# Second graph layer of a GNN kernel: own products moved into the loop of the neighbour sums, transposes two tiles later, the convolution spread over that loop, the output bias added later

## The chip, the cores and the metric

The kernel runs on one core of one Trainium2 chip. The metric is the device time of one execution in microseconds (us). The core has a matrix engine (TensorE, PE in the profile), a vector engine (VectorE, DVE), a scalar engine (ScalarE, ACT), GpSimd (POOL) and a queue that issues transfers (SyncE, SP). Each engine takes its own instructions strictly in the order of the program and waits for the others by semaphores.

## The reference, cut to what matters

The whole program is a graph layer, an attention and expert layer, a second graph layer and a second attention layer over 1250 nodes of width 512. The change touches the second graph layer and what prepares the second attention. In reduced form:

```
h   = layernorm(x)
own = h @ W_self.T
agg = A @ (h @ W_neigh.T) / deg            # A: 1250 x 1250 counts of edges
u   = own + agg + bias1
x   = x + layernorm(u) * gamma + beta
g   = layernorm(x)                         # second attention layer
c   = g + conv3(g, pos_w) + pos_b          # along the nodes, per channel
q, k, v = split(c @ qkv_w.T + qkv_b)
x   = x + attention(q, k, v) @ wo_w.T + wo_b
```

Everything is float32. The sums with A are exact in a split form: `h @ W_neigh.T` is kept as two parts, nb_hi and nb_lo, whose sum is the value.

## The kernel before, in words

The nodes lie in T = 10 tiles of P = 125 rows, the 512 channels in K = 4 blocks of 128. X holds x by rows. Four stages follow each other here; the times are those of the profiled execution.

1. The experts of the layer before (until 925 us) end with X complete.
2. The products loop (L1336 to L1347, 931 to 1007 us). A scheduler orders this part. For each tile: normalise a row tile (L639), transpose it on TensorE (L850), copy it out (L1341), multiply it by w_m and split the result into nb_hi (ScalarE, L646) and nb_lo (VectorE, L647), multiply it by w_s and add bias1 into the tile `slot` (L1347). GpSimd adds beta to X (L1339).
3. The sums' loop (L1414 to L1423, 1007 to about 1079 us), in an order written out by hand. In step t: ScalarE casts the counts of the next tile (cast1, L1359). TensorE sums 20 products of counts with nb_hi and nb_lo (adj_sum1, L861). VectorE joins the sum with the own product (L1365) and takes its statistics (L631 to L634). ScalarE takes the root (L635) and scales (L1375), and GpSimd multiplies by gamma and adds into X (scale1_, L1376 and L1377). The statistics and the normalisation of the finished X come two tiles later (stats1 and normed1), its transposition onto TensorE three tiles later (turn1_, L850 and L1393), with two copies of one column each by VectorE (L1397, L1398) that give every tile its neighbours' edge columns. GpSimd adds the output bias wo_b to X there (L1392). The convolution of tiles 0 and 1 (conv1: one ScalarE and two VectorE instructions for a channel block, L1407 to L1409) stands in step 5.
4. The projections (L1459 to L1466, until 1184 us): convolution of tiles 2 to 5, then q, k and v of tiles 0 and 1, convolution of tiles 6 to 9, then q, k and v of tiles 2 to 5 and of 6 to 9. TensorE's results go through three PSUM buffers (ps_mm); VectorE reads out q (L1443) and v (L1457), ScalarE and VectorE the two parts of k (L1449, L1450).

The second attention begins after that and takes the rest of the time. PSUM has three buffers for products (ps_mm), two for transposes (ps_tp) and two for sums (ps_o); the pool `work` keeps two of each of its tiles (h, u, the statistics). Weights share three SBUF buffers, so w_k and w_v of the second attention are loaded when w_m and w_s have been read for the last time.

Of the kernel before, what the change touches and what calls it, by code (L numbers as in the profile page):

```python
# [9 lines left out]
F32 = mybir.dt.float32  # L10
# [5 lines left out]
AF = mybir.ActivationFunctionType  # L16
ALU = mybir.AluOpType
# [3 lines left out]
P = 125  # L21
T = N // P
D = 512
K = D // 128
# [548 lines left out]
def tile_usual(ctx: ExitStack, tc: tile.TileContext, a: dict, out: bass.AP):  # L573
    nc = tc.nc
# [7 lines left out]
    def close(*pools):  # L582
        for p in pools:
            p.__exit__(None, None, None)
# [35 lines left out]
    X = keep.tile([P, T, D], F32, name="X")  # L620
    atu_pool, atu = pool("atu", 1, "left")

    CT = atu.tile([P, T, N], F16, name="CT")
    deg = keep.tile([P, T], F32, name="deg")
    edges = keep.tile([P, 1], F32, name="edges")

    def stats(pool, x):
        st = pool.tile([P, 6], F32, name="st")
        mv = pool.tile([P, 2], F32, name="mv")
        rs = pool.tile([P, 1], F32, name="rs")  # L630
        nc.vector.bn_stats(st, x)  # L631
# [3 lines left out]
        nc.scalar.sqrt(rs, rs)  # L635
        return mv, rs
# [35 lines left out]
    qk_b = cols(a["qk_b"], "qk_b")  # L672
    w_q = load_w(a["Wq"], "w_q")
# [58 lines left out]
    with (  # L732
# [73 lines left out]
        late, banks, touched, hs, hTs = [], {}, {}, {}, {}  # L806
# [9 lines left out]
        for r in range(rounds):  # L816
# [7 lines left out]
            while order and (order[0][0] <= r or r == rounds - 1):  # L824
                _, i, t = order.pop(0)
# [8 lines left out]
    def ps_mm():  # L834
        return psum.tile([128, 512], F32, tag="mm", name="ps_mm")
# [4 lines left out]
    def ps_o():  # L840
        return psum.tile([128, 512], F32, tag="o", name="ps_o", bufs=2)
# [4 lines left out]
    def transposed(x):  # L846

        ps = ps_tp()
        for k in range(K):
            nc.tensor.transpose(ps[:, k * P : (k + 1) * P], x[:, k * 128 : (k + 1) * 128], ident[:P, :P])  # L850
        return ps[:, : K * P].rearrange("p (k n) -> p k n", k=K)

    def product(ps, xT, t, w):

        for k in range(K):
            nc.tensor.matmul(ps, xT[:, k, span(t, t + 1)], w[:, k, :], start=(k == 0), stop=(k == K - 1))

    def summed(ps, ad):

        for n, (t, part) in enumerate((t, part) for t in range(T) for part in (nb_hi, nb_lo)):  # L860
            nc.tensor.matmul(ps, ad[:, t, :], part[:, t, :], start=(n == 0), stop=(n == 2 * T - 1))  # L861
# [177 lines left out]
    with (  # L1039
# [147 lines left out]
        for i in (1, 3):  # L1187
            r = slice(i * E, (i + 1) * E)
# [53 lines left out]
    with tc.tile_pool(name="moe", bufs=2, side="right") as moe:  # L1242
# [89 lines left out]

    slot = slots.tile([128, T, D], F32, name="slot")
    hT = slot[:, :, : K * (P + 2)].rearrange("p t (k n) -> p t k n", k=K)
    w_q = load_w(a["qkv"][:, :D], "w_q1")
    for t in range(T):  # L1336
        h = work.tile([P, D], F32, name="h")
        norm(h, X[:, t, :])
        nc.gpsimd.tensor_add(X[:, t, :], X[:, t, :], beta1)  # L1339
        xT = work.tile([128, K, P], F32, tag="xT4", name="hT1")  # L1340
        nc.scalar.copy(xT, transposed(h))  # L1341
        ps = ps_mm()
        product(ps[:P], xT, 0, w_m)
        split(nb_hi[:, t, :], nb_lo[:, t, :], ps[:P])
        ps = ps_mm()
        product(ps[:P], xT, 0, w_s)
        nc.vector.tensor_add(slot[:P, t, :], ps[:P], bias1)  # L1347
    w_k = load_w(a["qkv"][:, D : 2 * D], "w_k1")
    w_v = load_w(a["qkv"][:, 2 * D :], "w_v1")

    manual = tc.manual_schedule()
    manual.__enter__()
    xT = xc.tile([128, K, N], F32, name="xT")
    us, hs = {}, {}

    def cast1(t):
        if t < T:
            ads[t] = adj.tile([P, T, P], F32R, name="ad1")
            nc.scalar.copy(ads[t], CT[:, :, span(t, t + 1)])  # L1359

    def adj_sum1(t):
        agg = ps_o()
        summed(agg[:P], ads.pop(t))
        u = work.tile([P, D], F32, name="u")
        nc.vector.scalar_tensor_tensor(u, agg[:P], deg[:, t : t + 1], slot[:P, t, :], op0=ALU.mult, op1=ALU.add)  # L1365
        mv, rs = stats(work, u)
        us[t] = (u, mv, rs)

    def scale1_(t):
        if not 0 <= t < T:  # L1370
# [8 lines left out]
    def stats1(t):  # L1379
        if 0 <= t < T:  # L1380
            hs[t] = stats(work, X[:, t, :])

    def normed1(t):
        if 0 <= t < T:
            h = work.tile([P, D], F32, name="h")
            normed(h, X[:, t, :], *hs[t])
            hs[t] = h

    def turn1_(t):
        if not 0 <= t < T:  # L1390
            return
        nc.gpsimd.tensor_add(X[:, t, :], X[:, t, :], wo_b)  # L1392
        nc.scalar.copy(hT[:, t, :, 1 : P + 1], transposed(hs.pop(t)))  # L1393
        if t == 0:
            nc.vector.memset(hT[:, t, :, 0:1], 0.0)
        else:
            nc.vector.tensor_copy(hT[:, t, :, 0:1], hT[:, t - 1, :, P : P + 1])  # L1397
            nc.vector.tensor_copy(hT[:, t - 1, :, P + 1 : P + 2], hT[:, t, :, 1:2])  # L1398
        if t == T - 1:
            nc.vector.memset(hT[:, t, :, P + 1 : P + 2], 0.0)  # L1400

    def conv1(t0, t1):

        for k in range(K):
# [3 lines left out]
            nc.vector.scalar_tensor_tensor(c, at[:, :, :P], pos_w[:, k, 0:1], c, op0=ALU.mult, op1=ALU.add)  # L1408
            nc.vector.scalar_tensor_tensor(c, at[:, :, 2:], pos_w[:, k, 2:3], c, op0=ALU.mult, op1=ALU.add)  # L1409
# [3 lines left out]
    cast1(0)  # L1413
    for t in range(T + 3):  # L1414
        cast1(t + 1)
        if t < T:
            adj_sum1(t)
        stats1(t - 2)
        scale1_(t)
        normed1(t - 2)  # L1420
        turn1_(t - 3)
        if t - 3 == 2:
            conv1(0, 2)  # L1423
    close(work_pool, adj_pool, g1_pool, atu_pool)


    qkv1_pool, qkv1 = pool("qkv1", 1, "left")
# [3 lines left out]
    K2 = qkv1.tile([128, H, N], F32R, name="K2")  # L1431
    V = qkv1.tile([P, T, D], F32, name="V1")

    def project1_(t0, t1):
        n = (t1 - t0) * P
        for w in (w_q, w_k):
            for f in range(K):
                ps = ps_mm()
                for k in range(K):
                    nc.tensor.matmul(ps[:, :n], w[:, k, f * 128 : (f + 1) * 128], xT[:, k, span(t0, t1)],  # L1440
                                     start=(k == 0), stop=(k == K - 1))
                if w is w_q:
                    nc.vector.tensor_scalar(qT[:, f, span(t0, t1)], ps[:, :n], qk_b[:, f : f + 1],  # L1443
                                            float(D) ** -0.5, op0=ALU.add, op1=ALU.mult)
                    continue
                for i, (own, other) in enumerate(PAIRS):
                    hi, lo = (K2[r, 2 * f + i, span(t0, t1)] for r in (own, other))
                    b = qk_b[own, K + f : K + f + 1]
                    nc.scalar.activation(hi, ps[own, :n], AF.Identity, bias=b)  # L1449
                    nc.vector.scalar_tensor_tensor(lo, ps[own, :n], b, hi.bitcast(F32),  # L1450
                                                   op0=ALU.add, op1=ALU.subtract)
# [351 lines left out]
```

## Time and profile before

| what | value |
|---|---|
| time, median of 3 runs | 1625.26 us (1623.89 to 1626.26) |
| time of the profiled execution | 1624.99 us |
| its span from first to last instruction | 1623.1 us |
| TensorE busy | 1456.4 us, 90% |
| VectorE busy | 897.3 us, 55% |
| ScalarE busy | 706.6 us, 44% |
| GpSimd busy | 443.1 us, 27% |

The busy shares are means over stages with different limits. For this change the stretch from 931 us (first w_m product) to 1184 us (last v product) is what counts, and in it the time in which TensorE waits. A row of the timeline gives the start, the duration, the engine, the line, the operation with its tiles, and in brackets the idle time before it with what ended it. A float32 product of one tile appears as eight TensorE records.

### The profile page before, as it was taken

Reading aid. Unit: us, or ns where it says so; the run is one execution under the profiler, and the core shown is the slowest. Engines: PE = TensorE matmul, PEld = TensorE weight load, DVE = VectorE, ACT = ScalarE, POOL = GpSimd, SP = SyncE. Lnnn points to the kernel's source line nnn. Section 1 sums busy time; section 2 is a strip of 40 time slices with the busy share of each in tenths; the row PEclk is TensorE's granted clock in tenths of the full one; section 3 lists DMA queues with packets and bytes.
Section 4 is the critical chain, followed back from the end, with each engine's and each line's share of the span. In section 5 each row is a group of like instructions: output and inputs, shape, how many; then the busy total and the mean of one; then the engine's idle time right before and its main releaser. Section 6 shows DMA issues by size and latency. Waiting matters only on the chain. (4 is left out here: it accounts for less than half of the span.)

```text
span 1623.1 us, 21508 instructions
## 1 busy us (share of the span) xinstructions
PE 1456.4 (90%) x8133; PEld 954.3 (59%) x8133; DVE 897.3 (55%) x1413; ACT 706.6 (44%) x1334; POOL 443.1 (27%) x634
## 2 busy tenths in 40 slices
PE   4999998868888998999999899879978999999995
PEld 2566744447777776444444445654456777777773
DVE  5985556634433332411222332764278889999992
ACT  2333433335555553111100111432157888888882
POOL 0110000011111111000000010540057888887872
PEclk8999999979999999999999999989989999999998
DMA  4001000010101010010000201000100000000000
GB/s 133 25 1 52 1 1 1 0 42 16 40 15 44 19 25 14 29 50 26 26 26 27 83 0 52 1 0 1 36 16 14 14 20 20 21 20 21 20 8 22
DMA packets 41666, 39.82 MB, mean 25 GB/s; under 512 B 25717, under 2 KB 30063, under 8 KB 41553
## 3 DMA queue, kind: packets, MB, share of 16 engines
q1 hardware_dynamic: 41553, 38.36, 8.1%
q8 instruction: 66, 1.08, 0.3%
q14 instruction: 47, 0.39, 0.1%
HBM read 25.51 MB, written 2.56 MB: 17 GB/s over the span
## 5 line engine op out<-in xcount | busy, mean ns | idle before, releaser
L1573 POOL TENSOR_TENSOR e<-e,sg 125x1250 f32<-125x1250 f32 x80 | 206.0, 2576 | 34.3 <-ACT sg L1570 33.2
L1285 DVE SCALAR_TENSOR_TENSOR X<-ps_o,gate,X 125x512 f32<-125x512 f32 x80 | 60.1, 751 | 192.5 <-PE ps_o L1283 192.5
L1521 PE MATMUL S<-K,stacks 128*125 128x512 f32 (+1 forms) x480 | 126.0, 387 | 30.7 <-ACT sg L1570 29.9
L1583 PE MATMUL ps_t<-ident,e 125*125 125x125 f32 x800 | 135.6, 293 | 12.4 <-ACT R L1624 6.0
L1283 PE MATMUL ps_o<-we,hid 128*125 128x512 f32 x320 | 141.0, 595 | 0.0
L1590 ACT ACTIVATE pT<-ps_t 125x500 f32<-125x500 f32 x200 | 117.9, 589 | 47.8 <-PE ps_t L1583 46.9
L1583 PEld LDWEIGHTS ps_t<-ident,e 125*125 125x125 f32 x800 | 108.6, 191 | 48.0 <-ACT pT L1590 27.5
L1535 DVE MAX8 best<-S 125x8 f32<-125x1250 f32 x80 | 116.9, 1462 | 34.8 <-PE S L1521 33.5
L1275 PE MATMUL ps_mm<-yT,we 128*128 128x500 f32 (+1 forms) x352 | 127.6, 521 | 0.3 <-DVE gate L1183 0.3
L1278 ACT ACTIVATE hid<-ps_mm,b 128x500 f32<-128x500 f32 (+1 forms) x44 | 26.9, 611 | 220.6 <-PE ps_mm L1275 220.6
L1555 DVE MAX8 best<-rest 125x8 f32<-125x1250 f32 x80 | 117.1, 1464 | 2.8
L1546 DVE MATCH_REPLACE8 rest<-best,S 125x1250 f32<-125x1250 f32 x80 | 116.0, 1450 | 0.0
L1060 PE MATMUL S<-K,stacks 128*125 128x512 f32 (+10 forms) x288 | 87.1, 413 | 29.9 <-ACT e L1082 25.3
L1570 ACT ACTIVATE sg<-S,below 125x1250 f16<-125x1250 f32 x80 | 104.8, 1310 | 18.0 <-POOL below L1556 18.0
L1639 PE MATMUL O<-pT,V 125*64 125x125 f32 x1600 | 112.6, 279 | 0.0
L1521 PEld LDWEIGHTS S<-K,stacks 128*125 128x125 f32 x480 | 76.3, 193 | 52.1 <-ACT sg L1570 36.2
L1563 ACT ACTIVATE e<-S,nm 125x1250 f32<-125x1250 f32 x80 | 104.1, 1302 | 2.3 <-DVE rest L1546 1.1
L1108 ACT COPY pT<-ps_t 125x500 f32<-125x500 f32 (+3 forms) x112 | 54.9, 490 | 113.9 <-PE ps_t L1103 113.4
L1339 POOL TENSOR_TENSOR X<-X,beta 125x512 f32<-125x512 f32 x10 | 13.4, 1359 | 329.0 <-DVE h L639 328.3
L1275 PEld LDWEIGHTS ps_mm<-yT,we 128*128 128x128 f32 x352 | 66.9, 191 | 61.0 <-issue 58.6
L1283 PEld LDWEIGHTS ps_o<-we,hid 128*125 128x125 f32 x320 | 59.2, 187 | 71.6 <-issue 71.3
L990 POOL TENSOR_TENSOR stacks<-yT,stacks 64x125 fp32r<-64x125 f32 x80 | 34.1, 426 | 230.0 <-ACT stacks L989 226.6
(225 smaller groups left out, 2669.7 us busy)
## 6 DMA issues: line engine op xcount, KB each, us to landing
we<-in_W SPq DMA_DIRECT2D x16, 512.0 KB
stacks<-stacks SPq DMA_DIRECT2D x160, 31.2 KB
stacks<-stacks SPq DMA_DIRECT2D x40, 125.0 KB
X<-in_x SPq DMA_DIRECT2D x5, 500.0 KB
out<-y SPq DMA_DIRECT2D x10, 250.0 KB
w_n<-in_wn SPq DMA_DIRECT2D x1, 1024.0 KB
w_c<-in_wc SPq DMA_DIRECT2D x1, 1024.0 KB
w_q<-in_Wq SPq DMA_DIRECT2D x1, 1024.0 KB
```

The costliest lines, as they stand in the source:

```text
L1275: nc.tensor.matmul(ps[:, :n], w1[:, k, f * 128 : (f + 1) * 128], yT[:, k, span(t0, t1)], start=(k == 0), stop=(k == K - 1))
L1283: nc.tensor.matmul(ps[:P], hid[:, f, span(t, t + 1)], w2[:, f, :], start=(f == 0), stop=(f == FF // 128 - 1))
L1521: nc.tensor.matmul(score[n, a_][:, n0:n1], stacks[i][:, x, h, :], K2[:, h, n0:n1], start=(x == 0), stop=(x == 1))
L1535: nc.vector.max(out=top[:, 0:8], in_=score[n, a_][:, :N])
L1546: nc.vector.match_replace(out=rest, in_to_replace=top[:, 0:8], in_values=score[n, a_][:, :N], imm_value=LOWEST)
L1555: nc.vector.max(out=top[:, 8:16], in_=rest)
L1563: nc.scalar.activation(e, score[n, a_][:, :N], AF.Exp, bias=found[n, a_][0])
L1570: nc.scalar.activation(sg, score.pop((n, a_))[:, :N], AF.Sign, bias=found.pop((n, a_)), accum_out=signs[:, 2 * n + a_ : 2 * n + a_ + 1])
L1573: nc.gpsimd.tensor_mul(e, e, sg)
L1583: nc.tensor.transpose(turned[n, g][:P, span(b - g0, b - g0 + 1)], es[n, b // T][:, span(b % T, b % T + 1)], ident[:P, :P])
L1590: nc.scalar.activation(pTs[n][:, g0:g1, :], turned.pop((n, g))[:P, : (g1 - g0) * P].rearrange("p (t n) -> p t n", n=P), AF.Relu)
L1639: nc.tensor.matmul(outs[n][a_ * DH : (a_ + 1) * DH, :P], V[:, t, h * DH : (h + 1) * DH], pT[:, a_ * T + t, :], start=(t == 0), stop=(t == ...
```

## The change

The own product of a tile, h @ W_self.T, moves from the products loop into the sums' loop: the transposed tiles are kept for all ten tiles in `slot` (as inT), and own1(t) multiplies them just ahead of the sums of tile t and adds bias1 into u. The join of sum and own product (joined1) is a step of its own, at the end of the VectorE work of a step. In the sums' loop the statistics and the normalisation come one tile later (before: two), the transposition two tiles later (before: three). The edge columns are copied by ScalarE instead of VectorE. The convolution is called by channel blocks: blocks of tiles 0 and 1 in steps 4 to 7, three blocks of tiles 2 to 5 in steps 8 and 9, always ahead of the statistics of that step, the fourth block after the loop, and those of tiles 6 to 9 between the q projections of tiles 2 to 5. After the loop the projections of tiles 0 and 1 are placed between the last transposes. The ten additions of wo_b stand beside the projections of tiles 6 to 9. The load of w_v is issued ahead of that of w_k. The core of the diff:

```diff
     for t in range(T):
         h = work.tile([P, D], F32, name="h")
         norm(h, X[:, t, :])
         nc.gpsimd.tensor_add(X[:, t, :], X[:, t, :], beta1)
-        xT = work.tile([128, K, P], F32, tag="xT4", name="hT1")
-        nc.scalar.copy(xT, transposed(h))
+        nc.scalar.copy(inT[:, t, :, :], transposed(h))
         ps = ps_mm()
-        product(ps[:P], xT, 0, w_m)
+        product(ps[:P], inT[:, t, :, :], 0, w_m)
         split(nb_hi[:, t, :], nb_lo[:, t, :], ps[:P])
-        ps = ps_mm()
-        product(ps[:P], xT, 0, w_s)
-        nc.vector.tensor_add(slot[:P, t, :], ps[:P], bias1)
...
+    def own1(t):
+        ps = ps_mm()
+        product(ps[:P], inT[:, t, :, :], 0, w_s)
+        us[t] = work.tile([P, D], F32, name="u")
+        nc.vector.tensor_add(us[t], ps[:P], bias1)
...
+    def joined1(t):
+        u = us[t]
+        nc.vector.scalar_tensor_tensor(u, aggs.pop(t)[:P], deg[:, t : t + 1], u, op0=ALU.mult, op1=ALU.add)
+        us[t] = (u, *stats(work, u))
...
     def turn1_(t):
-        nc.gpsimd.tensor_add(X[:, t, :], X[:, t, :], wo_b)
         nc.scalar.copy(hT[:, t, :, 1 : P + 1], transposed(hs.pop(t)))
...
-            nc.vector.tensor_copy(hT[:, t, :, 0:1], hT[:, t - 1, :, P : P + 1])
-            nc.vector.tensor_copy(hT[:, t - 1, :, P + 1 : P + 2], hT[:, t, :, 1:2])
+            nc.scalar.copy(hT[:, t, :, 0:1], hT[:, t - 1, :, P : P + 1])
+            nc.scalar.copy(hT[:, t - 1, :, P + 1 : P + 2], hT[:, t, :, 1:2])
...
-    for t in range(T + 3):
-        cast1(t + 1)
-        if t < T:
-            adj_sum1(t)
-        stats1(t - 2)
-        scale1_(t)
-        normed1(t - 2)
-        turn1_(t - 3)
-        if t - 3 == 2:
-            conv1(0, 2)
+    for t in range(T):
+        cast1(t + 1)
+        own1(t)
+        turn1_(t - 2)
+        adj_sum1(t)
+        if 4 <= t < 8:
+            conv1(0, 2, t - 4)
+        elif t >= 8:
+            conv1(2, 6, *((0, 1) if t == 8 else (2,)))
+        stats1(t - 1)
+        normed1(t - 1)
+        joined1(t)
+        scale1_(t)
...
-    conv1(2, 6)
-    project1_(0, 2)
+    turn1_(T - 2)
+    project1_(0, 2, w_q, 0, 1)
+    conv1(2, 6, 3)
+    project1_(0, 2, w_q, 2, 3)
+    stats1(T - 1)
+    normed1(T - 1)
+    project1_(0, 2, w_k, 0)
+    turn1_(T - 1)
+    project1_(0, 2, w_k, 1, 2, 3)
     values1_(0, 2)
-    conv1(6, 10)
-    project1_(2, 6)
+    for f in range(K):
+        project1_(2, 6, w_q, f)
+        conv1(6, 10, f)
+    for f in range(K):
+        project1_(2, 6, w_k, f)
     values1_(2, 6)
-    project1_(6, 10)
+    for w in (w_q, w_k):
+        for f in range(K):
+            project1_(6, 10, w, f)
+            nc.gpsimd.tensor_add(X[:, f + 4 * (w is w_k), :], X[:, f + 4 * (w is w_k), :], wo_b)
+    for t in range(8, T):
+        nc.gpsimd.tensor_add(X[:, t, :], X[:, t, :], wo_b)
     values1_(6, 10)
```

The arguments after w in project1_ are the blocks f of 128 output channels.

More of the change, by code (lines that the diff above doesn't have):

```diff
@@ L1334, in tile_usual @@
     hT = slot[:, :, : K * (P + 2)].rearrange("p t (k n) -> p t k n", k=K)
+    inT = slot[:, :, : K * P].rearrange("p t (k n) -> p t k n", k=K)
     w_q = load_w(a["qkv"][:, :D], "w_q1")
@@ L1339, in tile_usual @@
         nc.gpsimd.tensor_add(X[:, t, :], X[:, t, :], beta1)
-        xT = work.tile([128, K, P], F32, tag="xT4", name="hT1")
-        nc.scalar.copy(xT, transposed(h))
+        nc.scalar.copy(inT[:, t, :, :], transposed(h))
         ps = ps_mm()
-        product(ps[:P], xT, 0, w_m)
+        product(ps[:P], inT[:, t, :, :], 0, w_m)
         split(nb_hi[:, t, :], nb_lo[:, t, :], ps[:P])
-        ps = ps_mm()
-        product(ps[:P], xT, 0, w_s)
-        nc.vector.tensor_add(slot[:P, t, :], ps[:P], bias1)
-    w_k = load_w(a["qkv"][:, D : 2 * D], "w_k1")
-    w_v = load_w(a["qkv"][:, 2 * D :], "w_v1")
+    w_k, w_v = (wpool.tile([128, K, D], F32, tag="w", name=name) for name in ("w_k1", "w_v1"))
+    for w, c in ((w_v, 2), (w_k, 1)):
+        nc.sync.dma_start(w, a["qkv"][:, c * D : (c + 1) * D].rearrange("(k p) f -> p k f", p=128))
     manual = tc.manual_schedule()
@@ L1353, in tile_usual @@
     xT = xc.tile([128, K, N], F32, name="xT")
-    us, hs = {}, {}
+    us, hs, aggs = {}, {}, {}
     def cast1(t):
@@ L1359, in cast1 @@
             nc.scalar.copy(ads[t], CT[:, :, span(t, t + 1)])
-    def adj_sum1(t):
[L1362 to L1367, printed above, removed]
+    def own1(t):
[3 more added lines that the diff above has]
+        nc.vector.tensor_add(us[t], ps[:P], bias1)
+    def adj_sum1(t):
+        aggs[t] = ps_o()
+        summed(aggs[t][:P], ads.pop(t))
+    def joined1(t):
+        u = us[t]
+        nc.vector.scalar_tensor_tensor(u, aggs.pop(t)[:P], deg[:, t : t + 1], u, op0=ALU.mult, op1=ALU.add)
+        us[t] = (u, *stats(work, u))
     def scale1_(t):
@@ L1396, in turn1_, with conv1 @@
         else:
-            nc.vector.tensor_copy(hT[:, t, :, 0:1], hT[:, t - 1, :, P : P + 1])
-            nc.vector.tensor_copy(hT[:, t - 1, :, P + 1 : P + 2], hT[:, t, :, 1:2])
+            nc.scalar.copy(hT[:, t, :, 0:1], hT[:, t - 1, :, P : P + 1])
+            nc.scalar.copy(hT[:, t - 1, :, P + 1 : P + 2], hT[:, t, :, 1:2])
         if t == T - 1:
             nc.vector.memset(hT[:, t, :, P + 1 : P + 2], 0.0)
-    def conv1(t0, t1):
-        for k in range(K):
+    def conv1(t0, t1, *ks):
+        for k in ks:
             c = xT[:, k, span(t0, t1)].rearrange("p (t n) -> p t n", n=P)
@@ L1412, in tile_usual @@
     nc.vector.tensor_scalar(pos_m, pos_w[:, :, 1], 1.0, None, op0=ALU.add)
-    cast1(0)
-    for t in range(T + 3):
-        cast1(t + 1)
-        if t < T:
-            adj_sum1(t)
-        stats1(t - 2)
-        scale1_(t)
-        normed1(t - 2)
-        turn1_(t - 3)
-        if t - 3 == 2:
-            conv1(0, 2)
-    close(work_pool, adj_pool, g1_pool, atu_pool)
-    qkv1_pool, qkv1 = pool("qkv1", 1, "left")
-    qT = qkv1.tile([128, K, N], F32, name="qT1")
-    K2 = qkv1.tile([128, H, N], F32R, name="K2")
@@ L1432, in tile_usual, with project1_ @@
-    V = qkv1.tile([P, T, D], F32, name="V1")
-    def project1_(t0, t1):
-        n = (t1 - t0) * P
[L1436 to L1451, printed above, removed]
+    def project1_(t0, t1, w, *fs):
+        n = (t1 - t0) * P
+        for f in fs:
+            ps = ps_mm()
+            for k in range(K):
+                nc.tensor.matmul(ps[:, :n], w[:, k, f * 128 : (f + 1) * 128], xT[:, k, span(t0, t1)],
+                                 start=(k == 0), stop=(k == K - 1))
+            if w is w_q:
+                nc.vector.tensor_scalar(qT[:, f, span(t0, t1)], ps[:, :n], qk_b[:, f : f + 1],
+                                        float(D) ** -0.5, op0=ALU.add, op1=ALU.mult)
+                continue
+            for i, (own, other) in enumerate(PAIRS):
+                hi, lo = (K2[r, 2 * f + i, span(t0, t1)] for r in (own, other))
+                b = qk_b[own, K + f : K + f + 1]
+                nc.scalar.activation(hi, ps[own, :n], AF.Identity, bias=b)
+                nc.vector.scalar_tensor_tensor(lo, ps[own, :n], b, hi.bitcast(F32),
+                                               op0=ALU.add, op1=ALU.subtract)
@@ L1457, in values1_ @@
             nc.vector.tensor_add(V[:, t, :], ps[:P], v_b)
-    conv1(2, 6)
-    project1_(0, 2)
-    values1_(0, 2)
-    conv1(6, 10)
-    project1_(2, 6)
-    values1_(2, 6)
-    project1_(6, 10)
+    cast1(0)
+    for t in range(T):
[11 more added lines that the diff above has]
+        scale1_(t)
+    close(adj_pool, g1_pool, atu_pool)
+    qkv1_pool, qkv1 = pool("qkv1", 1, "left")
+    qT = qkv1.tile([128, K, N], F32, name="qT1")
+    K2 = qkv1.tile([128, H, N], F32R, name="K2")
+    V = qkv1.tile([P, T, D], F32, name="V1")
+    turn1_(T - 2)
[6 more added lines that the diff above has]
+    turn1_(T - 1)
+    close(work_pool)
+    project1_(0, 2, w_k, 1, 2, 3)
+    values1_(0, 2)
+    for f in range(K):
[3 more added lines that the diff above has]
+        project1_(2, 6, w_k, f)
+    values1_(2, 6)
+    for w in (w_q, w_k):
[4 more added lines that the diff above has]
+        nc.gpsimd.tensor_add(X[:, t, :], X[:, t, :], wo_b)
     values1_(6, 10)
```

## The prediction, made before the changed kernel ran

> **What bounds the kernel now.** I read the busy time by stage first, then TensorE's waits from the first sum to the second q projection, then the timeline engine by engine.
>
> ```profile
> span 1623.1 us, 21508 instructions
> 931.00:1007.00 76.00, 75.81 (x200) 34.72 (x198) 22.34 (x51) 12.38 (x28) 11.98 (x10) 0.98 0.02 7
> 1007.00:1082.00 75.00, 57.70 (x247) 44.57 (x246) 51.73 (x141) 29.30 (x56) 38.60 (x30) 0.91 0.06 23
> ...
> PE ps_tp L850 <- DVE h L639: 12.3, 4, 4.5
> PE ps_o L861 <- ACT ad L1359: 5.0, 4, 2.9
> PE ps_mm L1440 <- DVE qT L1443: 1.4, 1, 1.4
> ...
> 1070.61 0.65 PE L850 MATMUL ps_tp<-ident,h 125*128 125x125 f32 x4 [4.45 <-DVE h L639]
> 1074.92 1.09 PE L850 MATMUL ps_tp<-ident,h 125*128 125x125 f32 x4 [3.67 <-DVE h L639]
> 1078.22 1.10 PE L850 MATMUL ps_tp<-ident,h 125*128 125x125 f32 x4 [2.20 <-DVE h L639]
> 1079.11 6.42 PE L1440 MATMUL ps_mm<-xT,w_q 128*128 128x250 f32 x24
> ```
>
> The columns of a window are its length, then busy time of PE, weight loads, DVE, ACT, POOL, then the clock. In the products loop TensorE is full and VectorE busy 22 of 76 us. In the sums' loop VectorE is busy 52 of 75 us, TensorE waits and its clock falls to 0.91. The three waits add up to 18.7 us; the largest are at the end, where the last three transposes wait for normalised rows with nothing else to do. The q run of 24 takes 6.42 us, against 5.18 at the 0.216 us a record of the run of 32 that follows (6.91 us): the slow clock is paid too. Later, from 1088 to 1184 us, TensorE is full.
>
> **TensorE's part of the change.** An own product is eight records in 3.43 us (x8 rows of w_s start 3.43 us apart), so ten move: 34.3 us. From the first w_m product (931.35) to the first q product of tiles 2 to 5 (1102.30) is 171.0 us now. At full clock, without waits, the same work is: products loop 76.0 - 34.3 = 41.7; sums' loop 10 x (3.43 own + 4.72 sum) + 8 x 0.36 for transposes = 84.4; behind it 2 x 0.36 + 8 x 1.73 for q and k of tiles 0 and 1 + 6.87 for v = 21.4. Sum 147.5: at most 23.4 us can be won. A step of the sums' loop is 8.51 us.
>
> The products loop keeps TensorE as its bound: a pair of tiles is 8.1 us of it, and VectorE needs 2 x (1.2 statistics + 0.5 to 1.2 row + 0.69 split) = 4.8 to 6.2. Its other partners are under 3 us a pair. I cost it at nothing; were the cover gone, each us over 8.1 would count five times.
>
> **The new chain from tile to tile.** In the changed order VectorE does in a step: bias add, convolution, statistics and row of tile t-1, join and statistics of tile t. The rows for it:
>
> ```profile
> 1011.30 0.75 DVE L1365 SCALAR_TENSOR_TENSOR u<-ps_o,deg,slot 125x512 f32<-125x512 f32 x1 [3.02 <-PE ps_o L861]
> 1013.85 0.81 ACT L1375 ACTIVATE u<-u,nm__6589,rs 125x512 f32<-125x512 f32 x1 [0.23 <-DVE nm__6589 L1374]
> 1014.74 1.29 POOL L1376 TENSOR_TENSOR u<-u,gamma 125x512 f32<-125x512 f32 x1 [33.50 <-ACT u L1375]
> 1016.11 1.28 POOL L1377 TENSOR_TENSOR X<-X,u 125x512 f32<-125x512 f32 x1
> ...
> 1076.00 0.68 DVE L631 BATCH_NORM_STATS2 st<-X 125x6 f32<-125x512 f32 x1
> 1077.62 0.55 DVE L639 TENSOR_SCALAR h<-X,mv,rs 125x512 f32<-125x512 f32 x1 [0.33 <-ACT rs L635]
> ...
> 1042.81 1.52 POOL L1377 TENSOR_TENSOR X<-X,u 125x512 f32<-125x512 f32 x1
> 1043.24 1.36 DVE L1409 SCALAR_TENSOR_TENSOR xT<-slot,pos_w,xT 128x250 f32<-128x250 f32 x1
> 1044.53 1.48 DVE L1408 SCALAR_TENSOR_TENSOR xT<-slot,pos_w,xT 128x250 f32<-128x250 f32 x1
> 1046.44 0.48 DVE L1408 SCALAR_TENSOR_TENSOR xT<-slot,pos_w,xT 128x250 f32<-128x250 f32 x1
> 1073.65 1.22 DVE L639 TENSOR_SCALAR h<-X,mv,rs 125x512 f32<-125x512 f32 x1 [0.33 <-ACT rs L635]
> ```
>
> Call J(t) the start of the join. X(t) is complete at J + 6.15 (1011.30 to 1017.39 and a hand-over). Statistics and row take 2.08 more until VectorE is free (1076.00 to 1078.08). So J(t+1) is at least J(t) + 8.23, under TensorE's 8.51: up to step 3 the chain hides.
>
> From step 4 the convolution stands ahead of the statistics. ScalarE first scales tile t-1 (from J + 2.55), casts (from 3.27), copies the transposed rows (4.41 to 4.97), copies two edges and runs the convolution's activation. The ScalarE edge copy is not in the trace: below, 0.1 us (the pace of its small roots back to back); above, 1.23, the longest of the VectorE copies it replaces. The nearest row is a root of 125x1, 0.20 us; I take two starts 0.1 apart, activation done at 5.81. VectorE could then do its two instructions of 250 columns at 5.85, 0.91 for both, and begin the statistics at 6.76.
>
> Against that: POOL adds X from 4.81 to 6.09. The rows at 1043.24 and 1044.53 took 1.36 and 1.48 us beside POOL, the one at 1046.44 0.48. The Trainium skill (SBUF — State Buffer, Who interferes with whom) says that a VectorE instruction with two inputs in SBUF fully blocks against a GpSimd instruction that reads SBUF, and that one with a single such input, outside the two-port modes, does not. It speaks against this placing: by it the pair waits to 6.09 and the statistics begin at 7.00; without it at 6.76. I take 7.00: J(t+1) = J + 9.08, in steps 4 to 7.
> In step 8 four instructions of 500 columns (1.42 a pair) run from 6.1 to 8.94, so 11.02. In step 9 there is no cast; the pair is ready at 4.92 but blocked to 6.1, over at 7.52: 9.60.
>
> The sum: J(3) = 931.35 + 41.7 + 4 x 8.15 + 2 x 0.36 = 1006.4; + 4 x 9.08 + 11.02 + 9.60 = J(9) = 1063.3. TensorE alone would be there at 1057.5. Its loss of 5.8 us shows ahead of the transposes of tile 7 (own product and sum of step 9 around it, about 1.4) and of tile 8 (about 4.4, no cover left).
>
> **Behind the loop.** After 4.4 us of waiting the clock is low, as at 1078: transposes 0.9 instead of 0.36, the q run of 24 6.42 instead of 5.18. q ends at J(9) + 9.0, the first k block at 10.75. VectorE's queue holds the q read-outs ahead of the last statistics: they start at about 9.5, after the last read-out, then 1.61, and the row 1.22 rather than 0.55, since the ten additions of wo_b follow X(9) on GpSimd without waiting for the projections they stand beside (6.15 to about 19 us; the row at 1073.65 is this case). Row at 12.3, a wait of 1.6 for tile 9. Then 0.4 + 5.19 + 6.87: first q product of tiles 2 to 5 at J(9) + 24.9 = 1088.2, against 1102.3: 14.1 us earlier.
>
> The clock is the second place for a rule. The skill (TensorE: Matmul & The Clock Gate, Part 1) lets the clock fall only after an idle window of about 3.4 us. By that the 1.4 us and 1.6 us cost only themselves. The trace is harsher: after 2.03 + 1.01 us within 4 us (1050 to 1054) eight sums took 3.52 instead of 1.86 us. By the trace up to 1.7 more would go if both were followed by it; I add nothing and keep it for the range.
>
> **What I cost at nothing.** Casts leave TensorE's path: cast(t+1) ends at about J + 4.5, eight us ahead of its sum (if not, 0.5 to 2.9 us each, as now). Moved wo_b: 13 us of GpSimd beside full TensorE; between 0 and the 0.7 above. w_k now waits for w_s until own1(9), at 1052; now both loads are over 8 us after the first issue (1004.15 to 1012), and k is needed at 1072. On SP nothing waits behind it but the far w_o. Convolution of tiles 6 to 9: 1.42 us of VectorE in q steps of 3.36 us that use 0.74. The attention follows unchanged.
>
> Profiled 1624.99 - 14.1 = 1610.9; the median is 0.27 above that execution, so 1611.
>
> **Rivals.**
> 1. The chain stays hidden: no blocking by POOL and short ScalarE work. Then 8.84, about 11.0 and 8.4 in those steps, and a warm clock; waits shrink to 0 to 4 us of the 9.3: 1602 to 1607. For it: with 8.23 against 8.51 little is missing. Against: the two blocked rows.
> 2. The waits only change their place: each hand-over of steps 4 to 9 costs 1 to 2 us more than I put (edge copies of 0.3 to 0.9, both instructions of a pair blocked), plus cold clocks. Six times 1 to 2: 1617 to 1623. For it: all in one queue. Against: 0.20 us for the nearest small ScalarE row.
> 3. Slower. The edge copies on ScalarE stand on the chain in steps 4 to 9, twelve of them. It decides at (14.1 + 3.3) / 12 = 1.45 us above my 0.1 each: at 1.6 us the time is 1629. For it: VectorE's copies took up to 1.23 us. Against: that was POOL's blocking, the uncontended ones took 0.17.
> 4. It doesn't do what it says: if the own products in the new place found TensorE waiting for the same rows, nothing would be won: 1625. Against: they read tiles kept since the products loop.
>
> **The numbers.** My case 0.68, 1606 to 1616 by itself; rival 1 0.14; rival 2 0.11; rival 3 0.04; rival 4 0.03. About 0.2% (3.3 us) is what a measurement can tell from no change: rival 2's upper end, 1622 to 1623, and rival 4 fall within it. Faster 0.91, within 0.04, slower 0.05. The range 1602 to 1618 holds my case, most of rival 1 and the low end of rival 2.
>
> **What would show it.** Products loop about 42 us long; no wait of the sums for casts; transposes waiting only for tiles 7, 8 and 9, the longest ahead of tile 8; joins 8.5 us apart at first, about 9.1, 11 and 9.6 later; convolution rows of 250 columns longer than 0.48 us; full TensorE from the q of tiles 2 to 5. Wrong if the products loop shows waits for rows, if joins spread beyond 10 us in steps 4 to 7, or if TensorE waits in the later projections.

## The result, and the profile after

The changed kernel takes 1610.62 us (median of 4 runs, 1608.29 to 1611.85) against 1624.58 us for the kernel before (4 runs, 1623.78 to 1626.26) on the same chip: a ratio of 0.9911, 95% interval 0.9894 to 0.9928. The profiled execution took 1611.85 us. The forecast was 1611.

Single runs of one kernel lie up to about 0.5% from their median, and much of that arises before the stage that is changed (its first w_m product lay anywhere from 929.4 to 936.0 us in the kernels below, whose code is the same up to there). The length of the changed stage repeats far better, 156.98 and 156.95 us in two executions of the changed kernel (the kernel before was profiled once). So I compare stages: from the first w_m product to the first q product of tiles 2 to 5.

| | before | after |
|---|---|---|
| first w_m product | 931.35 | 932.10 |
| first q product of tiles 2 to 5 | 1102.30 | 1089.08 |
| stage | 170.95 | 156.98 |
| TensorE busy in it | 152.08 | 149.31 |
| TensorE idle in it | 18.87 | 7.67 |
| of that, waits for normalised rows, casts and a q read-out | 18.7 | 6.5 |

The stage is 13.97 us shorter. Three views of the changed kernel say how. First the page's head and the busy time by stage, with the columns as before (length, then PE, weight loads, DVE, ACT, POOL, then the clock):

```profile
span 1610.1 us, 21469 instructions
PE 1454.7 (90%) x8133; PEld 954.3 (59%) x8133; DVE 892.6 (55%) x1395; ACT 710.3 (44%) x1352; POOL 442.4 (27%) x634
...
932.00:974.00 42.00, 40.81 (x115) 19.25 (x114) 16.84 (x41) 11.18 (x27) 11.11 (x9) 0.96 0.00 1
974.00:1064.00 90.00, 85.19 (x316) 55.43 (x315) 51.02 (x127) 30.61 (x65) 23.26 (x18) 0.99 0.07 24
1064.00:1089.00 25.00, 23.32 (x86) 17.19 (x86) 12.40 (x26) 10.06 (x22) 15.89 (x12) 0.91 0.00 1
```

TensorE has the same 8133 matmul records as before; no work was saved, it was moved under waits. Of the 13.97 us, 11.2 are idle time that is gone, and 2.8 are busy time: the same products, with less of the stage at the low clock. The products loop is now 42 us, the sums' loop has TensorE busy 85 of 90 us at a clock of 0.99, where it was busy 58 of 75 at 0.91. The low clock is left only from tile 8's wait on. The waits and the rows behind them:

```profile
PE ps_tp L850 <- DVE h L639: 6.5, 3, 4.1
...
1053.94 0.65 PE L850 MATMUL ps_tp<-ident,h 125*128 125x125 f32 x4 [0.72 <-DVE h L639]
1063.32 1.10 PE L850 MATMUL ps_tp<-ident,h 125*128 125x125 f32 x4 [4.08 <-DVE h L639]
1064.21 9.09 PE L1422 MATMUL ps_mm<-xT,w_q 128*128 128x250 f32 x32
1076.66 0.65 PE L850 MATMUL ps_tp<-ident,h 125*128 125x125 f32 x4 [1.68 <-DVE h L639]
1089.08 13.58 PE L1422 MATMUL ps_mm<-xT,w_q 128*128 128x500 f32 x32
```

No wait for casts (5.0 us before) and none for the q read-out (1.4) is left. The transposes of tiles 7, 8 and 9 alone wait. The 32 q records take 9.09 us after the wait of 4.08, where 32 at full clock are 6.9. Last, one step in the middle of the loop, around the convolution; its join stood at 1007.27:

```profile
1012.15 1.28 POOL L1382 TENSOR_TENSOR X<-X,u 125x512 f32<-125x512 f32 x1
1013.16 0.55 DVE L1412 SCALAR_TENSOR_TENSOR xT<-slot,pos_w,xT 128x250 f32<-128x250 f32 x1 [1.76 <-ACT xT L1411]
1013.75 0.48 DVE L1413 SCALAR_TENSOR_TENSOR xT<-slot,pos_w,xT 128x250 f32<-128x250 f32 x1
1014.14 0.69 DVE L631 BATCH_NORM_STATS2 st<-X 125x6 f32<-125x512 f32 x1
```

X is complete at 1013.43, yet its statistics (fourth row) start only when the two sums of the convolution, which stand ahead of them in VectorE's order, are through, 6.87 us after the join. That is the chain that the prediction described, with the next join 8.89 us after this one.

### The profile page after: what moved, and what is told of

The parts are those of the page before. It is cut to its first block, busy times and chain, and to the rows that moved or that the text cites. A ratio compares the mean times of both kernels' runs of the same rounds, so it can differ in the third digit from the quotient of the medians.

```text
span 1610.1 us, 21469 instructions
## 1 busy us (share of the span) xinstructions
PE 1454.7 (90%) x8133; PEld 954.3 (59%) x8133; DVE 892.6 (55%) x1395; ACT 710.3 (44%) x1352; POOL 442.4 (27%) x634
## 5 line engine op out<-in xcount | busy, mean ns | idle before, releaser
L1607 PE MATMUL ps_t<-ident,e 125*125 125x125 f32 x800 | 136.3, 294 | 12.4 <-ACT R L1648 6.0
```

Of the source, the lines that this page charges most:

```text
L1607: nc.tensor.transpose(turned[n, g][:P, span(b - g0, b - g0 + 1)], es[n, b // T][:, span(b % T, b % T + 1)], ident[:P, :P])
```

## The experiments

Four questions: which part brings the time, what the convolution's place costs and why, what the output bias is worth, and whether the waits that are left can be had. J(t) is the start of the join of tile t, and a hand-over is the distance from one join to the next.

**The own products alone.** The kernel before, with the own products in the sums' loop and nothing else (w_v is loaded ahead of w_k there too, as w_s is now read longer):

```diff
     def adj_sum1(t):
+        ps = ps_mm()
+        product(ps[:P], inT[:, t, :, :], 0, w_s)
+        u = work.tile([P, D], F32, name="u")
+        nc.vector.tensor_add(u, ps[:P], bias1)
         agg = ps_o()
         summed(agg[:P], ads.pop(t))
-        u = work.tile([P, D], F32, name="u")
-        nc.vector.scalar_tensor_tensor(u, agg[:P], deg[:, t : t + 1], slot[:P, t, :], op0=ALU.mult, op1=ALU.add)
+        nc.vector.scalar_tensor_tensor(u, agg[:P], deg[:, t : t + 1], u, op0=ALU.mult, op1=ALU.add)
```

> The kernel before with one part of the change: the own products move into the sums' loop, everything else stays (three tiles to the transposes, edges on VectorE, wo_b in the loop, convolution and projections behind the loop). Theory (TensorE's waits inside the loop are filled, the tail needs the other parts): the loop's waits of 7.0 us (0.55 + 0.51 + 2.90 + 2.03 + 1.01) and about 1.7 us of slow clock go, the three waits behind the last sum (4.45 + 3.67 + 2.20) stay: about 8.7 us faster than before, 1616. Rival A (the gain lies in the new order behind the loop, the own products are neutral): 1624 to 1626. Rival B (the own products alone bring it all): 1611.

Measured: 1614.31 us, ratio 0.992 (0.9899 to 0.9941); the stage is 161.70 us, 9.25 shorter than before. TensorE's waits in it:

```profile
PE ps_tp L850 <- DVE h L639: 9.7, 3, 3.8
PE ps_mm L1441 <- DVE qT L1444: 1.4, 1, 1.4
PE ps_mm L856 <- ACT slot L1341: 1.2, 4, 0.3
```

The waits for casts and the one for a row inside the loop are gone: the own products stand in them. The 9.7 us that are left are the three tail transposes, behind the loop, where no own product is to be had. From J(9) on the stage is as before (35.89 us, 35.88 before): the whole 9.25 us are won in the loop, as the theory said (8.7). That is two thirds of the stage's gain, so rival B (all of it) falls by the stage; the median alone, with this interval, would not rule it out.

**Everything but the own products.** The changed kernel with the own products back in the products loop:

```diff
-        own1(t)
         turn1_(t - 2)
...
-        u = us[t]
-        nc.vector.scalar_tensor_tensor(u, aggs.pop(t)[:P], deg[:, t : t + 1], u, op0=ALU.mult, op1=ALU.add)
+        u = work.tile([P, D], F32, name="u")
+        nc.vector.scalar_tensor_tensor(u, aggs.pop(t)[:P], deg[:, t : t + 1], slot[:P, t, :], op0=ALU.mult, op1=ALU.add)
```

> The changed kernel with the own products put back into the products loop; all other parts stay. Theory (the shorter lag is only affordable because 3.43 us of own product stand ahead of each transpose): TensorE needs only 5.1 us for a step, but the chain from join to join needs 8.23 us, 8.89 in steps 4 to 7, then 10.98 and 9.38 as measured in the changed kernel. J(9) comes at 1012 + 3 x 8.25 + 4 x 8.89 + 10.98 + 9.38 = 1093, the second q projection 25.9 later at 1119 against 1102 before: about 16 us slower than before, 1641. Rival A (the order behind the loop carries the gain): faster than before, 1612 to 1620. In the trace the theory wants a TensorE wait for the row ahead of every transpose, about 3 us each.

Measured: 1636.51 us, ratio 1.0072 (1.0043 to 1.0101): slower than before. The stage is 185.09 us, 14.14 longer. Its waits from the first w_m product to the q projections:

```profile
PE ps_tp L850 <- DVE h L639: 27.7, 10, 4.2
```

All ten transposes wait. The hand-overs are 8.13, 8.20, 8.26, 8.87, 8.86, 8.88, 8.87, 10.97 and 9.37 us, in steps 4 to 9 within 0.03 of the whole change's. So those are the length of the chain over VectorE, ScalarE and GpSimd, whatever TensorE has to do. With a lag of one tile every step takes a whole chain; the 5 us of TensorE's work in a step do not fill it, and with the 3.4 us of an own product they nearly do. The rest of the change costs 14 us of stage alone (the theory had 16) and saves 5 (161.70 - 156.98) beside the own products.

**The edge copies back on VectorE.** The changed kernel with one edit:

```diff
-            nc.scalar.copy(hT[:, t, :, 0:1], hT[:, t - 1, :, P : P + 1])
-            nc.scalar.copy(hT[:, t - 1, :, P + 1 : P + 2], hT[:, t, :, 1:2])
+            nc.vector.tensor_copy(hT[:, t, :, 0:1], hT[:, t - 1, :, P : P + 1])
+            nc.vector.tensor_copy(hT[:, t - 1, :, P + 1 : P + 2], hT[:, t, :, 1:2])
```

> The changed kernel with the two edge copies of a tile back on VectorE. Theory: the first copy waits for GpSimd's addition into X (about 0.9 us instead of 0.17), so from step 3 the statistics begin later: 0.3 to 0.5 us for each of steps 4 to 9 and about 0.2 of slack used up in step 3, together 2 to 3 us over the changed kernel, 1613. Rival C (ScalarE's copies cost as much on its queue): no difference, 1610 to 1611.

Measured: 1612.13 us, ratio 0.9909 (0.9884 to 0.9935); stage 159.61, 2.6 longer than with ScalarE. The two copies of a step on VectorE:

```profile
1011.74 1.13 DVE L1401 COPY slot<-slot 128x4 f32<-128x4 f32 x1 [0.99 <-ACT slot L1397]
1012.79 0.16 DVE L1402 COPY slot<-slot 128x4 f32<-128x4 f32 x1
```

A copy of four elements a partition takes 1.13 us while GpSimd's addition into X runs (until 1012.85) and 0.16 after it; on ScalarE each took 0.20. The hand-overs of steps 4 to 7 are 9.14 to 9.16 instead of 8.89, less than the 0.3 to 0.5 of the theory, and up to J(9) the stage is 0.9 us longer. The other 1.7 lie behind the loop and are no cost of the copies as such: after a wait of 2.58 us ahead of tile 9 (1.68 in the changed kernel) the granted clock was 0.50 for 3.4 us, and the 24 k products there took 6.92 us instead of 5.23. The medians do not tell this kernel from the changed one; the stage does.

**The whole convolution behind the scale.** The changed kernel, with the calls of conv1 after scale1_ instead of ahead of stats1:

```diff
-        if 4 <= t < 8:
-            conv1(0, 2, t - 4)
-        elif t >= 8:
-            conv1(2, 6, *((0, 1) if t == 8 else (2,)))
         stats1(t - 1)
         normed1(t - 1)
         joined1(t)
         scale1_(t)
+        if 4 <= t < 8:
+            conv1(0, 2, t - 4)
+        elif t >= 8:
+            conv1(2, 6, *((0, 1) if t == 8 else (2,)))
```

> The changed kernel with the convolution moved from ahead of the statistics to the end of each step, behind the join and the scale. Theory (the convolution on VectorE ahead of the statistics is what lengthens the chain from 8.23 to 8.89 and more): joins 8.5 apart in steps 4 to 7, bound by TensorE, and about 9.5 behind the four instructions of step 8; TensorE's waits ahead of the transposes of tiles 7 and 8 shrink from 4.8 to 1 to 2 us; 2 to 4 us faster than the changed kernel, 1607 to 1609. Rival D (GpSimd's multiplication and addition now meet the convolution and are blocked for as long): hand-overs stay at 8.9, 1610 to 1612.

Measured: 1613.17 us, ratio 0.9917 (0.9887 to 0.9946); stage 157.26 us, 0.3 longer. My theory had it shorter by 2 to 4 and falls; the rival, which had hand-overs of 8.9, came near. A step of it (join at 1017.19):

```profile
1020.69 1.30 POOL L1381 TENSOR_TENSOR u<-u,gamma 125x512 f32<-125x512 f32 x1 [5.84 <-ACT u L1380]
1022.07 1.35 POOL L1382 TENSOR_TENSOR X<-X,u 125x512 f32<-125x512 f32 x1
...
1021.14 1.13 DVE L1412 SCALAR_TENSOR_TENSOR xT<-slot,pos_w,xT 128x250 f32<-128x250 f32 x1 [1.43 <-ACT xT L1411]
1022.30 1.39 DVE L1413 SCALAR_TENSOR_TENSOR xT<-slot,pos_w,xT 128x250 f32<-128x250 f32 x1
```

ScalarE's row of the convolution comes after its scaling, so the two sums meet the multiplication by gamma and the addition, and take 1.13 and 1.39 us instead of 0.48. They delay the bias addition and the statistics behind them; the four hand-overs behind them are 9.03 to 9.04 us, and the one behind the four sums of step 8 is 10.97 where the theory had 9.5. What counts for the two sums is less their place in the step than what GpSimd does beside them.

**The convolution split.** ScalarE's row stays ahead of the statistics (1.7 us pass there until its next instruction), and the two sums go behind nm, the last small VectorE instruction ahead of the scaling, where VectorE is free and GpSimd not yet at work. conv1 is cut into its two halves, centre1 for ScalarE and sides1 for VectorE. Steps 8 and 9 take one block of 500 columns each, the third goes behind w_k's second block:

```diff
+        block = (0, 2, t - 4) if t < 8 else (2, 6, t - 8)
+        if t >= 4:
+            centre1(*block)
         stats1(t - 1)
         normed1(t - 1)
         joined1(t)
         scale1_(t)
+        if t >= 4:
+            sides1(*block)
...
-    project1_(0, 2, w_k, 1, 2, 3)
+    project1_(0, 2, w_k, 1)
+    conv1(2, 6, 2)
+    project1_(0, 2, w_k, 2, 3)
```

> The changed kernel, with the convolution split: its ScalarE row stays ahead of the statistics, its two VectorE sums go behind the line that folds the mean into the first layer norm's scale (nm), where VectorE is free from J+2.52 to J+3.44 and POOL's multiplication has not begun; steps 8 and 9 take one block of 500 columns each, the third block goes among the key projections of tiles 0 and 1. Theory (a late hand-over in steps 4 to 9 is VectorE's order, the pair of sums standing between X and its statistics): statistics start when POOL's addition ends, J+6.2, the row h is done at J+8.2, and the join follows TensorE, 8.5 us in every step instead of 8.89 four times, 10.98 and 9.38; J(9) comes 4.9 us earlier, the wait before tile 8's transposes goes from 4.08 to under 0.5; first w_m product to first q product of tiles 2 to 5 about 152 us instead of 156.98, time about 1606. Rival (the pair only changes places, as with the whole convolution behind the scale): the sums meet POOL's multiplication and hold up the bias addition or the statistics, a hand-over stays near 9 us, 156 to 158 us, time 1610 to 1612.

Measured: 1602.2 us, ratio 0.9867 (0.9845 to 0.9888), beside the changed kernel's 1611.37, 0.9918 (0.9899 to 0.9938), on the same chip (below). Stage 151.32 us, 5.7 shorter. A step of it (join at 1020.11), then its waits up to the q projections, then the two TensorE rows at the end of the loop:

```profile
1022.54 0.47 DVE L1414 SCALAR_TENSOR_TENSOR xT<-slot,pos_w,xT 128x250 f32<-128x250 f32 x1
1023.05 0.48 DVE L1415 SCALAR_TENSOR_TENSOR xT<-slot,pos_w,xT 128x250 f32<-128x250 f32 x1
...
1023.61 1.30 POOL L1381 TENSOR_TENSOR u<-u,gamma 125x512 f32<-125x512 f32 x1 [5.83 <-ACT u L1380]
...
1026.31 0.70 DVE L631 BATCH_NORM_STATS2 st<-X 125x6 f32<-125x512 f32 x1 [2.08 <-POOL X L1382]
```

```profile
PE ps_tp L850 <- DVE h L639: 2.2, 2, 2.0
PE ps_mm L856 <- DVE K L1440: 0.7, 1, 0.7
```

```profile
1062.82 0.65 PE L850 MATMUL ps_tp<-ident,h 125*128 125x125 f32 x4 [0.19 <-DVE h L639]
1063.30 6.92 PE L1430 MATMUL ps_mm<-xT,w_q 128*128 128x250 f32 x32
```

The sums take 0.47 and 0.48 and are over before GpSimd begins; the statistics now wait for X itself. All hand-overs from the third on are 8.50 to 8.52 us: TensorE's own time in every step. The wait of 4.08 us before tile 8 is 0.19, and the q run behind it takes 6.92 us instead of 9.09. That pairs the slow clock with the wait. Up to J(9) the stage is 4.4 us shorter: the hand-overs give 4.85, and its products loop happened to be 0.5 longer, ahead of the edit. Of the 4.85, 1.5 come from steps 4 to 7, where only the place of the sums differs, 2.5 from step 8 and 0.9 from step 9. In step 8 there is also one block of sums less than in the changed kernel, so what the place alone is worth there is not separated. Behind J(9) the stage is 1.3 shorter, mostly the 2.2 us of the clock less what is new, 0.70 for the k read-out and 0.35 more before tile 9.

**The output bias in the loop.** The changed kernel with the ten additions of wo_b back in turn1_:

```diff
     def turn1_(t):
+        nc.gpsimd.tensor_add(X[:, t, :], X[:, t, :], wo_b)
         nc.scalar.copy(hT[:, t, :, 1 : P + 1], transposed(hs.pop(t)))
...
-            nc.gpsimd.tensor_add(X[:, f + 4 * (w is w_k), :], X[:, f + 4 * (w is w_k), :], wo_b)
-    for t in range(8, T):
-        nc.gpsimd.tensor_add(X[:, t, :], X[:, t, :], wo_b)
```

> The changed kernel, with the output bias back in the loop (one POOL addition of 1.27 us in every turning step, instead of ten behind the loop). Theory (this part is worth next to nothing): POOL is free 5.8 us of every step, so the addition lies ahead of the gamma multiplication and only VectorE rows beside it feel it; the last normalised row behind the loop takes 0.55 instead of 1.32 us, so 0 to 1 us faster or slower, first w_m product to first q product of tiles 2 to 5 between 156.0 and 158.0 us. Rival (the part carries a gain): the addition in the loop pushes POOL's chain or meets the convolution sums in every step, hand-overs of steps 4 to 7 rise from 8.89 to above 9.2 us, 159 us or more.

Measured: 1614.37 us, ratio 0.9932 (0.991 to 0.9953); stage 160.58 us, 3.6 longer, hand-overs of steps 4 to 7 9.76 to 9.82 us. The theory (worth next to nothing) falls, the rival (159 us or more) holds:

```profile
1025.58 1.46 POOL L1397 TENSOR_TENSOR X<-X,wo_b 125x512 f32<-125x512 f32 x1
...
1025.94 1.38 DVE L1414 SCALAR_TENSOR_TENSOR xT<-slot,pos_w,xT 128x250 f32<-128x250 f32 x1
1027.24 0.68 DVE L631 BATCH_NORM_STATS2 st<-X 125x6 f32<-125x512 f32 x1
```

GpSimd is free for six of nine us, but it runs this addition as soon as the previous one ends, at the one moment when the second convolution sum stands ahead of the statistics, and the sum takes 1.38 us instead of 0.48. Behind the loop 1.9 us are won back (J(9) to the q product 24.02 us, 25.90 in the changed kernel), where the last row now takes 0.55 us as expected. That an engine has free time says nothing of where its next instruction will fall.

**Without the multiplication by gamma.** This kernel leaves the multiplication by gamma in the loop out of the computation. The values that reach the second attention are then others and the program behind this stage takes far longer (4145.8 us in all), so only the stage is read.

```diff
-        nc.gpsimd.tensor_mul(u, u, gamma)
         nc.gpsimd.tensor_add(X[:, t, :], X[:, t, :], u)
```

> The changed kernel without the multiplication by gamma in the loop (that multiplication is left out of the computation). Two readings of the 8.89 us hand-over in steps 4 to 7 and the 10.98 of step 8. Theory: in steps 4 to 7 the pair of sums waits for ScalarE (scale, cast, transposed copy, edges, centre row), not for POOL: hand-overs stay within 0.15 of 8.89. In step 9 the first row of 500 columns took 1.71 us beside POOL's addition: without the multiplication the addition lies earlier, the row takes about 0.75, the hand-over of the last step goes from 9.38 to about 8.5. Rival (POOL's chain of 2.6 us sets the pace in all of these steps): hand-overs of steps 4 to 7 fall to TensorE's 8.5 us. Time 1608 to 1610 by the theory, 1605 to 1607 by the rival.

Measured: hand-overs of steps 4 to 7 8.81 to 8.83 (8.89 with gamma), 10.98 in step 8 (10.98), 8.42 in the last (9.38). First a middle step (join at 1020.06), then the last step's first sum:

```profile
1023.55 1.29 POOL L1381 TENSOR_TENSOR X<-X,u 125x512 f32<-125x512 f32 x1 [7.52 <-ACT u L1380]
...
1025.94 0.48 DVE L1411 SCALAR_TENSOR_TENSOR xT<-slot,pos_w,xT 128x250 f32<-128x250 f32 x1 [2.07 <-ACT xT L1410]
1026.45 0.48 DVE L1412 SCALAR_TENSOR_TENSOR xT<-slot,pos_w,xT 128x250 f32<-128x250 f32 x1
...
1062.44 0.74 DVE L1411 SCALAR_TENSOR_TENSOR xT<-slot,pos_w,xT 128x500 f32<-128x500 f32 x1 [1.85 <-ACT xT L1410]
```

X is complete at 1024.84 and the pair still starts 5.88 us after the join: it waits for ScalarE. In the middle steps GpSimd's blocking is worth 0.07 us, in the last 0.96, as that row takes 0.74 instead of 1.71. The theory holds for the hand-overs. Its 1 to 3 us of gain do not show even in the stage, which is 157.69 us, 0.7 longer: up to J(9) it is 0.8 shorter, behind it 1.5 longer, as after a wait of 2.40 us ahead of tile 9 the granted clock was 0.50 for 3.4 us and 24 k products took 6.92 us instead of 5.23.

**The changed kernel again**, beside the three before:

> The changed kernel as it is, on the same chip as the split convolution: 1610 to 1613 us, ratio to the kernel before 0.990 to 0.993, and 157 us from the first w_m product to the first q product of tiles 2 to 5, by every theory; a difference from the other run of it is the spread of one run.

Measured: 1611.37 us, ratio 0.9918 (0.9899 to 0.9938), stage 156.95 us, the hand-overs within 0.02 us of the first.

**The split convolution again.** The first run's median lay 9.2 us under the changed kernel's, its stage 5.7.

> The kernel with the split convolution once more. In its first run the stage was 5.7 us shorter than the changed kernel's while the median was 9.2 us lower, and the profiled execution was the slowest of six. If the gain is the stage's alone, the profile again shows 151 us from the first w_m product to the first q product of tiles 2 to 5 and the time lies at 1604 to 1607; if more is gained elsewhere, the time is 1600 to 1603 again and the profile has a second stage that is shorter than the changed kernel's by 2 us or more.

Measured: 1603.31 us, ratio 0.9872 (0.9853 to 0.9892), stage 151.29 us. Both expectations are half met: the median is between them, and no second stage is shorter (from the q of tiles 2 to 5 to the end 520.9 us, with the changed kernel 521.0). The two profiled executions of this kernel lie 7.9 and 6.3 us above the medians, and lost 3.9 and 3.5 us ahead of the stage against that of the changed kernel. So some 5.7 of the 8 to 9 us are located; the remaining 2 to 3 are within what executions differ by, and stay open.

**The output bias on VectorE.** The split convolution, with the ten additions on VectorE at the same places of the program:

```diff
-            nc.gpsimd.tensor_add(X[:, f + 4 * (w is w_k), :], X[:, f + 4 * (w is w_k), :], wo_b)
+            nc.vector.tensor_add(X[:, f + 4 * (w is w_k), :], X[:, f + 4 * (w is w_k), :], wo_b)
     for t in range(8, T):
-        nc.gpsimd.tensor_add(X[:, t, :], X[:, t, :], wo_b)
+        nc.vector.tensor_add(X[:, t, :], X[:, t, :], wo_b)
```

> The kernel with the split convolution, and the ten additions of the output bias on VectorE instead of GpSimd, at the same places in the program, between the projections of tiles 6 to 9. Theory (the additions on GpSimd run at once behind the loop and block the VectorE rows with two SBUF inputs there): the last normalised row takes 0.55 instead of 1.61 us, the late convolution rows 0.74 instead of 1.80 and 1.63, the wait of 0.70 us for the k read-out goes and the wait before tile 9's transposes falls from 2.03 to about 1.0; the stage is 149.6 us instead of 151.3. The additions themselves stand in VectorE's idle time beside full TensorE (ten times 0.7 us in a stretch in which it is busy 29 of 82 us) and cost nothing. Rival (they delay the read-outs of q, k and v there): TensorE shows waits for PSUM buffers in the projections of tiles 6 to 9, and what the stage wins is lost there; no difference from the split convolution in all.

Measured: 1605.48 us, ratio 0.9885 (0.9866 to 0.9905); stage 148.84 us, 2.5 shorter again, of which 2.0 lie behind J(9) (22.62 us, 24.61 before this edit) and 0.5 in the products loop, ahead of the edit. Its last normalised row, and all of TensorE's waits from the first w_m product to the first instruction of the second attention:

```profile
1067.14 0.55 DVE L639 TENSOR_SCALAR h<-X,mv,rs 125x512 f32<-125x512 f32 x1 [0.27 <-ACT rs L635]
...
PE ps_mm L856 <- ACT slot L1341: 1.2, 4, 0.3
PE ps_tp L850 <- DVE h L639: 1.2, 2, 1.0
PE S L1556 <- ACT stacks L1541: 0.8, 1, 0.8
```

The theory's rows hold (0.55 instead of 1.61, no wait for k, 1.0 before tile 9), and the projections of tiles 6 to 9 show no wait, so the rival's reason fails. The time doesn't follow: the median is 2.2 us above the split convolution's, with overlapping intervals. In the profiled execution the attention takes 1.4 us longer (from its first product, 1162.27, to the end 440.3 us, against 438.9 with the changed kernel); whether that is this edit or spread is open. The stage has 2.4 us of waits left in 148.84; the split convolution, in either form, is the fastest kernel here, 1.1 to 1.3% under the kernel before.

## Why the prediction was right, step by step

The time was right, and so was the mechanism. Two terms of the sum were mis-sized by about 1 us each, in opposite directions; that they cancelled, and the forecast met the result within 0.4 us, is luck.

- **Products loop.** 41.7 predicted, 41.77 measured (932.10 to 973.87). Its partners were costed at nothing, and nearly so it was: its only waits are four of 0.30 us, one for each pair of tiles after the first.
- **Steps 1 to 3.** Bound by TensorE, as predicted (8.15 without a transpose, 8.51 with one): 8.23, 8.37, 8.51, and no wait of TensorE in them.
- **Steps 4 to 7.** Predicted 9.08, measured 8.89, 8.89, 8.88, 8.89. The mis-sized term is the blocking by GpSimd: I let the pair start at J + 6.09, when the addition into X ends, and put 0.24 us on each step. The pair was ready at 5.89 (5.85 predicted), and counted back from its end it ran freely from J + 5.96, 0.20 us before the record of the addition ends (6.16). Then 5.96 + 0.91 = 6.87, which is where the statistics start. Without blocking at all a step is 8.82 (8.81 to 8.83 in the run without gamma), so the term is 0.07. Rival 1, 8.84 in these steps, had these hand-overs; it did not have the time, as step 9 took 9.38 instead of its 8.4 and the clock did not stay warm.
- **Steps 8 and 9.** 11.02 and 9.60 predicted, 10.98 and 9.38 measured. The difference in step 9 is mostly that 0.20 us again; there the blocking is real (1.71 us for a sum of 0.74). The rule of the Trainium skill (SBUF — State Buffer, Who interferes with whom) thus held for the sums, which have two inputs in SBUF, and also for the k read-out (L1432), which has one: it took its 0.47 to 0.48 us while GpSimd's bias additions ran (1076.64 to 1082.64). What I had wrong is how much of a GpSimd record blocks.
- **The waits.** Tile 7: about 1.4 predicted, 0.72 measured. Tile 8: 4.4 and 4.08. Tile 9: 1.6 and 1.68. Tile 7's is the smaller because four hand-overs of 0.19 us less came before it.
- **Behind the loop.** J(9) to the first q product of tiles 2 to 5: 24.9 predicted, 25.90 measured. The mis-sized term is the clock after tile 8's wait: I took over what the slow clock had cost the q run in the trace of before (6.42 us for 24 records, then 1.73 for the rest: 8.15 in all), and the run took 9.09 us. The cost is no matter of 24 or 32 records but of how long the granted clock stays at 0.50. Before, that was until about 1081.5, 2.4 us into the q run; here until 1068.6, 4.4 us into it, and the records after that ran at full clock. A row of the kernel before, then two of the changed kernel (the clock is the third number from the end):

```profile
1081.00:1082.00 1.00, 1.00 (x5) 0.84 (x5) 0.96 (x2) 1.00 (x3) 0.00 (x0) 0.74 0.00 0
...
1068.00:1069.00 1.00, 1.00 (x5) 0.88 (x4) 0.27 (x1) 0.09 (x1) 0.98 (x1) 0.70 0.00 0
1069.00:1070.00 1.00, 1.00 (x7) 0.89 (x6) 0.04 (x1) 0.00 (x0) 1.00 (x2) 1.00 0.00 0
```

  VectorE's last read-out of q and with it the last statistics came at J + 10.55 instead of 9.5. The last row took 1.32 (1.22 predicted), blocked by the bias additions:

```profile
1069.24 10.94 POOL L1487 TENSOR_TENSOR X<-X,wo_b 125x512 f32<-125x512 f32 x8
...
1075.29 1.32 DVE L639 TENSOR_SCALAR h<-X,mv,rs 125x512 f32<-125x512 f32 x1 [0.27 <-ACT rs L635]
```

- **The clock.** I followed the trace for the cold run and added nothing after the waits of 1.4 and 1.6 us. That held: after 1.68 us the rest of k and v took 12.4 us (1076.66 to 1089.08), the 0.4 + 5.19 + 6.87 of full clock. The wait of 4.08 us is long enough also by the skill's rule (TensorE: Matmul & The Clock Gate, Part 1), so this kernel does not decide between the two. Two experiments do: waits of 2.58 us (edges on VectorE) and 2.40 us (no gamma) were followed by the slow clock, though both are shorter than the idle window of about 3.4 us that the rule wants. The measurement decides; what it gives in the rule's place stands at the end.
- **Costed at nothing.** Casts, w_k and w_v, the convolution of tiles 6 to 9 and the attention (438.9 us from its first product to the end, 438.7 before) cost nothing, as put; no wait of TensorE lies between 1090 and 1168 us. The moved wo_b lengthened the last row by 0.77 us (1.32 against 0.55), about the 0.7 that I named as its upper bound. What I didn't ask is what it would have cost unmoved: 3.6 us, by the run above. An edit that looks like housekeeping is worth a quarter of the stage's gain.
- **Edge copies.** Taken 0.1 us apart, measured 0.10 to 0.11, 0.20 each; the case for slower, which needed 1.45 us more for each, is out. So is rival 4: the own products fill waits, 9.25 us of them alone.

## What to carry to other kernels

When an engine waits in a loop, look for its own work without dependencies in a neighbouring loop and move it there: here 34.3 us of TensorE moved, and the loop grew by 15 us (75 to 90). A reordering that makes every step a whole chain pays only with such work beside it: alone it was 14 us slower. And before placing a VectorE instruction of the kinds that GpSimd held up here, see what GpSimd does at that moment, not how busy it is: with the same two sums a step took 8.89 us in one gap, 9.03 in another, and TensorE's own 8.51 in a third.

## What the runs showed of the hardware

- A blocked convolution sum came free 0.20 us before the end of the GpSimd record that blocked it. The sum's end less the duration of an unblocked one, and the end of the GpSimd record, are 1013.23 and 1013.43 in the changed kernel, 1021.79 and 1021.99, 1023.21 and 1023.42 with the convolution behind the scale, 1026.84 and 1027.04 with the bias in the loop, 1059.73 and 1059.93 in step 9.
- Two kinds of VectorE instruction with a single tensor input in SBUF were held up as well: the copy of four elements a partition (1.13 us against 0.16) and the normalisation of a row (L639, 1.32 us against 0.55). On ScalarE the same copy took 0.20 us beside GpSimd.
- Work without dependencies runs where it stands in its engine's order and not beside its neighbours in the program: the bias additions written between the projections of tiles 6 to 9 (from 1129.6 us) ran at 1069 to 1082 us.
- Between 945 and 1112 us, in every run, the granted clock was 1.00 or 0.50, and each slow phase lasted 3.4, 6.8 or 10.2 us. Cutting each trace into stretches of 3.41 us, counted from the start of a slow phase, and adding up TensorE's idle time in each, gives this. At full clock, the stretches with 2.19 us of idle time or more (2.19, 2.20, 2.40 and up) were followed by a slow one, and those with 1.81 us or less (1.81, 1.71, 1.70 and down) were not. So the place of a wait counts beside its length: one of 2.98 us, in the run of everything but the own products, fell on two stretches (1.14 and 1.81 us of idle time) and slowed nothing, while those of 2.58 and 2.40 us above did.
